# A two-layer graph network on one core: in the second layer a block's accumulator, query and softmax weights are placed in PSUM

## The chip, the core and the metric

The kernel runs on one NeuronCore of a Trainium2 chip. The engines have the names of the profile: PE multiplies matrices (PEld is its weight load), DVE (VectorE) and ACT (ScalarE)[...], POOL (GpSimd) here only issues DMAs, SP (SyncE) issues plain DMAs. The metric is the device time of one execution in microseconds. A change counts as measured here when it is above about 0.3%, and a verdict of faster or slower takes 2%.

## What is computed

Two graph layers over 6250 nodes and 100000 edges, with 128 channels, 8 heads of 16 channels, 16 node types and 32 edge types, then a linear map and a layer norm. Of one layer, this matters here:

```python
k, q, v = typed_linear(x, ntype, Wk), typed_linear(x, ntype, Wq), typed_linear(x, ntype, Wv)   # per node
kT = einsum('nhd,htdo->nhto', k, Watt); vT = einsum('nhd,htdo->nhto', v, Wmsg)                # per node and edge type
a = einsum('ehd,ehd->eh', kT[src, :, etype], q[dst]) * pri[:, etype].T / SQRT_D                # per edge and head
att = edge_softmax(a, dst, n)                                                               # over the edges of a node
hag = segment_sum(vT[src, :, etype] * att[:, :, None], dst)                                     # per node
h = silu(typed_linear(hag, ntype, Wa)); h = h * alpha + x * (1 - alpha); h = layernorm(h) * g + b
```

## The kernel before, in words

**Tables.** For each layer a table `tabs[l]` in HBM has, for each pair of node and edge type, one row of 256 values: the 128 of kT and the 128 of vT. The table of layer 0 is made in a first stage. That of layer 1 is made piece by piece while layer 0 goes over its edges (`nodes`, `pieces_of`, `table_block`): PE multiplies into PSUM tiles called `tb`, each a pair of banks of 512 values, of which the pool `tps` (line 780) has three. ACT copies them to SBUF and POOL scatters them (line 1183). All scatters must have landed before the first row of layer 1 is fetched. In layer 1 nothing is put into `tb`.

**Blocks and chunks.** Nodes are ordered by number of incoming edges and cut into 50 blocks of 128, one node a partition. Block b has KB[b] edge slots, and the blocks are grouped into 15 superblocks of 3 or 4 (`sbs`): 12 of one class of 4 node types each, and 3 mixed ones of all 16 types. A layer fetches 867 slots in all. Each fetch is an indirect DMA issued by POOL (line 966): it takes a column of 128 row numbers from the SBUF tile `ell` and brings 128 rows of 1 KB into `kv`. Four slots make a chunk; there are 12 buffers of a chunk.

**The order of the work** (`edges`, line 833). For each chunk of a block DVE multiplies the kT half by the block's query (line 978, `kv<-kv,q`) and sums each head's 16 products (line 982) into the scores `a`. Between these, one step of the generator `finished` runs, for the block before: scores masked (881), maximum (886), subtracted (888), exponential on ACT (890), sum (893), then chunk by chunk the vT half times its weight (901; the first chunk's product starts the accumulator `acc`), added to `acc` (908), and at the end the four partial sums of `acc` added up (911). Until then the `kv` buffers of the block before are held. So a block's rows are in use for about two blocks: with some 17 slots, or 5 chunks, in a block, about 10 of the 12 buffers.

After the last block of a superblock, `nodes` (line 1056) is spread as small pieces between the chunks: normalisation, typed linear map with masks `xm` made on DVE (line 232), tanh on ACT (line 1069), layer norm on DVE with a reciprocal root by iteration (1038 to 1042), and in layer 1 the final map and norm (1156 to 1169) and a scatter of the result by POOL (line 1216).

**Who sets the order.** POOL's queue is written out by hand (`manual_schedule(engines={Pool})`, line 1310); the instructions of the other engines are ordered by the framework's scheduler[...]. In layer 1 the queries come from HBM for a superblock at a time (`queries1`, line 827, tile `q` in SBUF), and `query(s, i)` (line 872) hands out the slice of a block, some chunks before that block starts.

In the kernel before, `q`, `a` (whose exponentials are written over the scores) and `acc` are SBUF tiles. So lines 978, 901 and 908 each have two SBUF inputs and one SBUF output.

## Time and profile before

| what | value |
|---|---|
| median of 3 runs | 3544.61 us (3541.61 to 3552.11) |
| the profiled execution | 3932.2 us, span 3930.4 us |
| first stage | 0 to 843 us |
| layer 0's edges (with the making of layer 1's table) | 843 to 2405 us |
| last scatters, nothing fetched | 2405 to 2497 us |
| layer 1's edges | 2497 to 3930 us |
| POOL over the span | 2104.1 us busy, 54% |
| DVE over the span | 2232.3 us busy, 57% |
| PE over the span | 1974.2 us busy, 50%, mean granted clock 0.697 |

How to read it: the profiled execution is longer than the timed ones, so its stages are compared with its own span, not with the median. The borders of the stages are the starts of the first fetch (line 966) of each layer and the last fetch of layer 0. "Busy" is the time in which an engine's records cover the clock; POOL's 0.30 us between two DMA issues is not in it. In the timeline, a row is start, duration, engine, line, operation, tiles, and in brackets the idle time before it and what ended it. Records of DVE overlap a little: one can start before the end of the one before.

### The profile page before, as it was taken

The numbers are of one execution on the slowest core, as the hardware profiler recorded it, in microseconds if no ns is written. First come the engines' busy times: TensorE is split into PE (matmuls) and PEld (weight loads), VectorE is DVE, ScalarE is ACT, GpSimd is POOL, SyncE is SP. The second block draws the span as 40 slices with busy tenths as digits, with TensorE's granted clock in tenths as the row PEclk, the third lists the DMA queues.
The fourth block names the chain that finished last, engine by engine and source line by source line (L and its number), as shares of the span: only waits on it lengthen the run. The fifth ranks groups of instructions, "written<-read, shape, count | busy, mean of one in ns | idle before, by whom it ended". The sixth has DMA issues, their size and how long they took to land. (4 is left out here: it accounts for less than half of the span.)

```text
span 3930.4 us, 25592 instructions
## 1 busy us (share of the span) xinstructions
PE 1974.2 (50%) x7142; PEld 887.1 (23%) x7142; DVE 2232.3 (57%) x4900; ACT 833.8 (21%) x1366; POOL 2104.1 (54%) x2032
## 2 busy tenths in 40 slices
PE   4999998950556367655766867202111122021212
PEld 2444553320222123222222323001010111010111
DVE  4787684424736456555745744346446465564746
ACT  1444434430123113421343144100000000000000
POOL 0000005637566566667556763476576676766764
PEclk9999999965667677677767777655555555555555
DMA  5676648793265346755566578533232233323321
GB/s 137 274 305 278 267 194 323 308 319 96 86 240 203 130 154 218 286 200 199 196 247 213 170 280 312 196 100 89 83 95 88 83 98 92 104 85 88 101 85 49
DMA packets 201147, 694.54 MB, mean 177 GB/s; under 512 B 61382, under 2 KB 111896, under 8 KB 175946
## 3 DMA queue, kind: packets, MB, share of 16 engines
q0 software_dynamic: 105424, 448.83, 34.2%
q1 hardware_dynamic: 72924, 234.11, 15.3%
q10 hardware_dynamic: 22642, 9.82, 1.1%
q8 instruction: 60, 0.98, 0.1%
q14 instruction: 97, 0.79, 0.1%
HBM read 268.12 MB, written 429.48 MB: 177 GB/s over the span
## 5 line engine op out<-in xcount | busy, mean ns | idle before, releaser
L966 POOL DMA_INDIRECT kv<-tab,ell x1734 | 1806.1, 1042 | 786.2 <-issue 501.0
L269 ACT COPY st<-tb 128x512 f32<-128x512 f32 (+1 forms) x976 | 683.1, 764 | 743.1 <-PE tb L262 458.4
L978 DVE TENSOR_TENSOR kv<-kv,q 128x512 f32<-128x512 f32 (+3 forms) x468 | 301.7, 647 | 469.2 <-DMA kv<-tab,ell 426.2
L732 PE MATMUL l<-xm,wkqv 128*128 128x512 f32 (+1 forms) x832 | 385.8, 599 | 54.8 <-DVE xm L232 54.8
L247 PE MATMUL nb<-ident,hag 128*128 128x128 f32 x100 | 25.4, 390 | 763.0 <-DVE hag L1014 350.1
L232 DVE SCALAR_TENSOR_TENSOR xm<-ntb,nb 128x384 f32<-128x384 bf16 (+1 forms) x336 | 186.7, 593 | 245.2 <-remote 158.4
L982 DVE TENSOR_REDUCE a<-kv 128x32 f32<-128x512 f32 (+3 forms) x468 | 297.2, 639 | 29.4 <-remote 6.5
L262 PE MATMUL tb<-bdv,kvT 32*128 32x512 f32 x800 | 276.5, 817 | 43.5 <-ACT st L269 24.8
L241 PE MATMUL nb<-xm,wa 128*128 128x384 f32 (+1 forms) x384 | 219.1, 731 | 151.2 <-DVE xm L232 91.0
L262 PE MATMUL tb<-bdk,kvT 32*128 32x512 f32 x800 | 256.4, 814 | 57.8 <-ACT st L269 35.5
L890 ACT ACTIVATE a<-a 128x128 f32<-128x128 f32 (+12 forms) x100 | 31.9, 319 | 1143.3 <-DVE a L888 487.1
L1183 POOL DMA_INDIRECT tab<-st,row x100 | 110.2, 1102 | 306.7 <-ACT st L269 265.7
L908 DVE TENSOR_TENSOR acc<-kv,acc 128x512 f32<-128x512 f32 (+3 forms) x368 | 233.2, 634 | 57.7 <-remote 47.6
L901 DVE TENSOR_TENSOR kv<-kv,a 128x512 f32<-128x512 f32 (+3 forms) x368 | 231.0, 636 | 0.0
L267 DVE COPY st<-tb 128x512 f32<-128x512 f32 (+1 forms) x208 | 149.2, 718 | 121.9 <-PE tb L262 88.4
L732 PEld LDWEIGHTS l<-xm,wkqv 128*128 128x128 f32 x832 | 149.0, 193 | 286.7 <-issue 199.1
L232 DVE SCALAR_TENSOR_TENSOR xm<-ntb,hT 128x512 f32<-128x512 int32 (+1 forms) x208 | 133.8, 658 | 139.7 <-PE l L732 102.1
L247 PE MATMUL nb<-ident,hs 128*128 128x128 f32 x100 | 32.1, 456 | 353.8 <-DVE hs L1094 274.9
L241 PE MATMUL nb<-xm,wq 128*128 128x384 f32 (+1 forms) x192 | 104.3, 704 | 179.4 <-DVE xm L232 159.1
L247 PEld LDWEIGHTS nb<-ident,hag 128*128 128x128 f32 x100 | 15.2, 193 | 781.7 <-issue 568.2
L720 POOL DMA_DIRECT2D ntb<-in_node_type_dram x13 | 7.3, 558 | 341.9 <-DVE xm L232 341.9
L262 PE MATMUL tb<-bdv,yT 32*128 32x512 f32 x784 | 169.7, 658 | 4.7 <-ACT st L269 3.5
(234 smaller groups left out, 2678.0 us busy)
## 6 DMA issues: line engine op xcount, KB each, us to landing
tab<-st SPq DMA_DIRECT2D x98, 2048.0 KB
kv<-tab,ell POOLq DMA_INDIRECT x1734
hr<-xrd SPq DMA_DIRECT2D x20, 192.0 KB
xrd<-xr POOLq DMA_DIRECT2D x11, 256.0 KB
hr<-in_x_dram POOLq DMA_DIRECT2D x10, 256.0 KB
ntb<-in_node_type_dram POOLq DMA_DIRECT2D x10, 256.0 KB
hr<-xrd SPq DMA_DIRECT2D x10, 256.0 KB
ntb<-typed SPq DMA_DIRECT2D x20, 96.0 KB
```

The lines of the kernel that those rows point to most:

```text
L232: nc.vector.scalar_tensor_tensor(xm[:, :n], ntb[:, :n], float(t), hT[:, :n], op0=ALU.is_equal, op1=ALU.mult)
L241: nc.tensor.matmul(ps[:, :n], w[:, t, :], xm[:, :n], start=(t == types[0]), stop=(t == types[-1]))
L262: nc.tensor.matmul(pt[:, b], yT[s, i * P:(i + 1) * P], bd[s, tt, :], start=True, stop=True)
L267: nc.vector.tensor_copy(to, pt)
L269: nc.scalar.copy(to, pt)
L732: nc.tensor.matmul(ps[i][:, :n], wkqv[:, i, t, :], xm[:, :n], start=(t == 0), stop=(t == TY - 1))
L901: nc.vector.tensor_tensor((v if j else acc).rearrange("p k (h d) -> p k h d", h=H), v.rearrange("p k (h d) -> p k h d", h=H), av[:, j0:j1, ...
L908: nc.vector.tensor_tensor(acc[:, :j1 - j0], kvt[j - 1][:, :j1 - j0, D:], acc[:, :j1 - j0], op=ALU.add)
L966: get = nc.gpsimd.indirect_dma_start(out=kv[:, j - j0, :], out_offset=None, in_=tabs[l][:], in_offset=bass.IndirectOffsetOnAxis(ap=ell[:, ...
L978: nc.vector.tensor_tensor(kk, kk, q.unsqueeze(1).to_broadcast([P, c, D]), op=ALU.mult)
L982: nc.vector.tensor_reduce(a[:, j0:j1, :], kk.rearrange("p k (h d) -> p k h d", h=H), axis=AX.X, op=ALU.add)
L1183: put = nc.gpsimd.indirect_dma_start(out=tabs[1].rearrange("(n t) c -> n (t c)", t=16), out_offset=bass.IndirectOffsetOnAxis(ap=row2[:, tg ...
```

## The change

It concerns layer 1 only (`l == 1`); layer 0 goes on as before. `query` takes a tile `tb` from the pool of bank pairs, [128, 2, 512] values, and has ACT copy the block's query into the first 128 values of its second bank. Line 978 reads the query from there. In `finished`, the exponentials are written behind the query in that bank (K times 8 values), not over the scores in SBUF; the sum of line 893 and the products of line 901 read them there. `acc` is the first bank of the pair. Nothing else differs: the same DVE instructions in the same number on the same sizes, and 50 more copies on ACT.

```diff
             def query(s, i):
-                return got[s][0][:, i, :]
-
-            def finished(s, i, chunks, kvt, a, sums, den):
+                if l == 0:
+                    return got[s][0][:, i, :], None
+                pair = tps.tile([P, 2, SB * P], F32, name="tb")
+                nc.scalar.copy(pair[:, 1, :D], got[s][0][:, i, :])
+                return pair[:, 1, :D], pair
+
+            def finished(s, i, chunks, kvt, a, pair, sums, den):
...
                 nc.vector.tensor_tensor(av, av, m.unsqueeze(1).to_broadcast([P, K, H]),
                                         op=ALU.subtract)
-                nc.scalar.activation(av, av, AF.Exp)
-                yield
-                yield
-                nc.vector.tensor_reduce(den[:, i, :], av.rearrange("p k h -> p h k"),
+                w = av if l == 0 else pair[:, 1, D:D + K * H].rearrange("p (k h) -> p k h", h=H)
+                nc.scalar.activation(w, av, AF.Exp)
+                yield
+                yield
+                nc.vector.tensor_reduce(den[:, i, :], w.rearrange("p k h -> p h k"),
                                         axis=AX.X, op=ALU.add)
 
-                acc = ep.tile([P, CH, D], F32, name="acc", bufs=1)
+                if l == 0:
+                    acc = ep.tile([P, CH, D], F32, name="acc", bufs=1)
+                else:
+                    acc = pair[:, 0].rearrange("p (k c) -> p k c", k=CH)
...
                         nc.vector.tensor_tensor(
                             (v if j else acc).rearrange("p k (h d) -> p k h d", h=H),
                             v.rearrange("p k (h d) -> p k h d", h=H),
-                            av[:, j0:j1, :].unsqueeze(3).to_broadcast([P, j1 - j0, H, HS]),
+                            w[:, j0:j1, :].unsqueeze(3).to_broadcast([P, j1 - j0, H, HS]),
                             op=ALU.mult)
...
             before = iter(())
-            q = query(0, 0)
+            q, pair = query(0, 0)
...
-                    before = finished(s, i, chunks, kvt, a, sums, den)
-                    q = then[0] if then else None
+                    before = finished(s, i, chunks, kvt, a, pair, sums, den)
+                    q, pair = then[0] if then else (None, None)
```

## The prediction

> **What bounds the kernel now.** The page's chain of waits breaks off after the last stores, so I read the sums by stage first, with borders at the first and last fetch of each layer. The change touches the last row alone.

> ```profile
> core 0: us, PE busy (x) PEld busy (x) DVE busy (x) ACT busy (x) POOL busy (x), PEclk, DMA share, GB/s
> 843.00:2405.00 1562.00, 916.04 (x2623) 377.32 (x2623) 879.63 (x1922) 417.60 (x554) 997.53 (x954) 0.70 0.58 200
> 2497.00:3931.00 1434.00, 256.51 (x642) 146.63 (x642) 803.28 (x2082) 46.03 (x126) 959.09 (x917) 0.53 0.31 89
> ```

> In the second layer (1434 us) the DMA engines are 31% busy, ACT hardly works, and POOL with 959 us is ahead of DVE with 803. Next, the groups of that stretch:

> ```profile
> L966 POOL DMA_INDIRECT kv<-tab,ell x867 | 905.6, 1045 | 402.4 <-issue 254.4 <-DVE acc L901 63.8 <-DVE hs L1083 15.1
> L1216 POOL DMA_INDIRECT out_dram<-o,node x50 | 53.5, 1070 | 73.8 <-DVE o L1169 61.0 <-issue 10.7 <-DVE a L888 0.9
> ...
> L978 DVE TENSOR_TENSOR kv<-kv,q 128x512 f32<-128x512 f32 x200 | 137.4, 687 | 250.3 <-DMA kv<-tab,ell 234.3 <-issue 15.9
> L982 DVE TENSOR_REDUCE a<-kv 128x32 f32<-128x512 f32 x200 | 135.3, 676 | 7.4 <-issue 2.1 <-remote 1.5 <-DVE m L886 1.3
> L908 DVE TENSOR_TENSOR acc<-kv,acc 128x512 f32<-128x512 f32 x150 | 102.7, 684 | 26.4 <-remote 24.1 <-issue 2.2
> ```

> POOL's account: 905.6 + 53.5 us in DMA records, 254.4 + 10.7 us of "issue" (0.30 us between two, the same everywhere), together 1224 us or 85% of the stretch; the other 210 us it waits, mostly for DVE to free `kv` (63.8 us, line 901) or to give a result (61.0 us, line 1169). DVE waits 234 us for fetched rows. So POOL's issue rate is the bound for most of the layer, with some stops that DVE causes.

> A fetch takes 1045 ns on average, but its median is 946. The timeline shows what the long ones are:

> ```profile
> 3209.64 0.68 DVE L901 TENSOR_TENSOR acc<-kv,a 128x512 f32<-128x512 f32 x1
> 3210.23 0.69 DVE L901 TENSOR_TENSOR kv<-kv,a 128x512 f32<-128x512 f32 x1
> 3210.31 3.23 POOL L966 DMA_INDIRECT kv<-tab,ell  x1 [0.30 <-issue]
> 3210.84 0.69 DVE L978 TENSOR_TENSOR kv<-kv,q 128x512 f32<-128x512 f32 x1
> 3211.44 0.69 DVE L901 TENSOR_TENSOR kv<-kv,a 128x512 f32<-128x512 f32 x1
> 3212.04 0.69 DVE L908 TENSOR_TENSOR acc<-kv,acc 128x512 f32<-128x512 f32 x1
> 3212.64 0.68 DVE L982 TENSOR_REDUCE a<-kv 128x32 f32<-128x512 f32 x1
> ...
> 3219.37 1.93 DVE L232 SCALAR_TENSOR_TENSOR xm<-ntb,nb 128x384 f32<-128x384 bf16 x4
> ...
> 3220.24 0.94 POOL L966 DMA_INDIRECT kv<-tab,ell  x1 [0.30 <-issue]
> ```

> The fetch that starts at 3210.31 lasts 3.23 us: to within 0.05 us until the row of DVE instructions with two SBUF inputs (lines 901, 978, 901, 908) gives way to the reduction of line 982 at 3212.64, plus an undisturbed 0.94. The fetch at 3220.24 starts amid four masks, which read one input from PSUM (`nb`), and takes 0.94. Over both layers I sorted the fetches and POOL's other indirect DMAs by what DVE did beside them: 126 beside only reductions (over 0.4 us) averaged 0.953 us, 61 beside masks (over 0.8 us) 0.970, 111 beside more than 1.3 us of two-input instructions 1.90. DVE's own instructions show no such stretching (line 978 lies between 675 and 709 ns).

> **The change, part by part.** *Removed: the stretching.* In the second layer 867 x (1045 - 946) ns = 86 us. All but some 6 us belong to lines 978, 901 and 908; other instructions still have two SBUF inputs (881, 888, 1014, 1090, 1094, the root's small ones). For each DMA start I took the remainder of the two-input row that it fell into: 226 us for all of them, 15 us for these others alone, so 15/226 of 86. Leaves 80 us of POOL's time.

> [...] By the rows it is 80 us; the 3.23 us fetch decides for the rows. A fetch takes its row numbers from SBUF (`ell`), which is a read.

> *What of the 80 us reaches the end.* I split all POOL DMAs of the layer (92 us over 946 ns, stores included): 47 us lie in 208 DMAs within 15 us after a stop of POOL, where DVE catches up in dense rows, and 45 us in the 709 others. The calm part counts in full: there DVE waits for rows. Of the other part some can be lost again in the next stop. So 45 to 86 in the profiled execution of 3932.2 us (span 3930.4); I take 70, making it about 3862. The timed runs are 388 us shorter. POOL's records and gaps are even, and its stops sum to some 620 us over both layers; so what is shorter there is likely the stops, and POOL is the bound for more of the time, which favours the upper end. With fewer stops there are fewer dense rows: the calm rate, 45/709 x 917, gives 58. I keep 70 for the median: 3545 - 70 = 3475.

> *Moved: operands to PSUM.* 752 DVE instructions get a PSUM operand: 234 of line 978, 234 of 901, 184 of 908, 50 each of 911 and 893. [...] The rows say nothing of it: line 1083 with a PSUM input takes 344 ns as line 1094 without does, line 1050 takes 286 from `nb` and 281 from `hs`: 0 to 4 us. I take the rows. No row shows DVE writing PSUM (234 instructions) or reading and writing the same bank (184 of line 908): above, I bound it by a doubling of the 0.60 us from start to start of two of them, 184 x 0.6 = 110 us; below, line 911 (1000 ns where line 982 needs 676 for as many values in unbroken order) might lose its 0.32 us, -16 us. I take 0, nearest to the rows with PSUM inputs. What hides it is DVE's 234 us of waiting for rows; without that cover it would count in full.

> *Added: 50 copies on ACT* (128x128), as long as the exponential of that size, 309 ns: 15 us on an engine with 46 of 1434 us busy. Its exponentials now write PSUM; no row shows ACT doing so. Bounds -5 and +5 us for 50 of them; I take 0, on an idle engine.

> *Added: a wait.* Line 978 of a block's first chunk waits for the copy. Behind it on DVE stands everything, and POOL waits for the buffers that DVE frees. The copy stands in ACT's queue behind tanh (line 1069) and the copy of line 1156, which wait for PE. Below nothing is excluded: it adds a step. Above: DVE's longest wait for tanh in this layer is 4.9 us (16.1 us in 6); once for each of 15 superblocks is 75 us of DVE. The query is asked for some steps before the block ends, and DVE has spare time, so I take 0. The bank pair itself is free: three pairs, two blocks in work, and the tables are finished before. POOL and SP queues get nothing new.

> **The rivals.**
> - *Freed (0.68):* as above, 3475; its own range 3445 to 3515.
> - *Swallowed (0.15):* POOL's stops for DVE (210 us) are set by DVE and PE, and grow by what the fetches save. For it: 47 of the 92 us lie behind such stops. Against: the 234 us that DVE waits for rows. Gives about 3540.
> - *Slower, by the copy's wait (0.11):* the copy is late at each block start. DVE's cover is 234 - 80 = 154 us; the gain is gone from (154 + 80)/50 = 4.7 us a block. At 6 us a block, 300 - 234 = 66 us are lost: about 3610. For it: ACT[...] waits up to 58 us for PE. Against: few of those waits have a query behind them.
> - *It does not do what it says (0.06):* an instruction with one input in PSUM still holds POOL off, because it reads and writes `kv` in place. Against: the masks' 0.970 us. Gives 3545.

> **How the numbers follow.** 0.3% (10.6 us) is about what a measurement of this kernel can tell from no change. Faster: all of the first and a little of the second, 0.71; within: 0.15; slower: the third and edges of the others, 0.14. The range 3445 to 3555 takes in the first case, the second and the fourth, and leaves out the slow one and the tails.

> **What would show it.** Right: in the second layer line 966 averages 950 to 965 ns, no fetch of 2 us or more beside lines 978, 901, 908, while the first layer keeps its long ones; that layer is 60 to 85 us shorter; lines 978 and 901 stay within 10 ns of 687. Swallowed: short fetches, but more than 250 us of POOL waiting for DVE. Slower: waits of line 978 for ACT's copy, several us long. Wrong in the sizes: line 908 far above 684 ns, or line 911 off its 1000.

## The result, and the profile after

The changed kernel takes 3498.2 us in the median of 4 runs (3493.8 to 3504.2), beside 3548.4 for the one before: ratio 0.9866, 95% interval 0.984 to 0.9892. By the ratio that is 47.5 us less, 38 to 57 by its interval: more than the 0.3% that this kernel's measurement can tell, though less than the 2% that counts as faster. 3475 had been predicted.

The first profile of before shows an execution that was held up for some 390 us: DVE and ACT each wait 384 us for updates of semaphores that came late (its rows with "<-remote", of which the later profiles have none). So the stages below are compared with a second profile of the same kernel, the first experiment. It had its own clean span, 3533.9 us. By stage, the second layer of the second profile of before, and then of after:

```profile
2273.00:3534.00 1261.00, 246.04 (x642) 145.74 (x642) 795.11 (x2082) 46.26 (x126) 931.18 (x917) 0.54 0.35 101
```

```profile
core 0: us, PE busy (x) PEld busy (x) DVE busy (x) ACT busy (x) POOL busy (x), PEclk, DMA share, GB/s
2286.00:3493.00 1207.00, 246.32 (x642) 145.66 (x642) 773.49 (x2082) 57.37 (x173) 874.21 (x917) 0.54 0.36 105
```

The last of the (x) pairs is POOL: 57.0 us less of it for the same 917 DMAs, and the stage is 54 us shorter. What runs ahead of that layer is left alone by the change; it took 2274 us in one profile and 2286 in the other, the first layer 1349 and 1355 of it. So the gain of the stage is POOL's, nearly one for one. The groups say of which instructions; POOL in the second layer of before (second profile), and of after, where line 966 has become 976:

```profile
L966 POOL DMA_INDIRECT kv<-tab,ell x867 | 877.0, 1011 | 284.9 <-issue 248.4 <-DVE acc L901 8.5 <-DVE acc L908 3.4
L1216 POOL DMA_INDIRECT out_dram<-o,node x50 | 54.2, 1084 | 46.6 <-DVE o L1169 32.0 <-issue 11.3 <-DVE a L982 1.5
```

```profile
L976 POOL DMA_INDIRECT kv<-tab,ell x867 | 823.5, 950 | 284.2 <-issue 243.2 <-DVE tb L911 7.6 <-DVE ri L1052 4.4
L1226 POOL DMA_INDIRECT out_dram<-o,node x50 | 50.7, 1014 | 50.1 <-DVE o L1179 35.4 <-issue 10.1 <-DVE rd L1019 1.5
```

A fetch fell from 1011 to 950 ns, which is the undisturbed 946 but for 4. POOL's idle time has hardly grown, from 331.5 us to 334.3: what the fetches save is not waited away. Now DVE: four of its groups before (second profile), then the same stretch of after. Lines 988, 992, 911, 918 and 921 are the former 978, 982, 901, 908 and 911; `tb` is the bank pair.

```profile
L978 DVE TENSOR_TENSOR kv<-kv,q 128x512 f32<-128x512 f32 x200 | 138.1, 690 | 414.1 <-DMA kv<-tab,ell 395.6 <-issue 18.3
L908 DVE TENSOR_TENSOR acc<-kv,acc 128x512 f32<-128x512 f32 x150 | 102.1, 681 | 0.0
L901 DVE TENSOR_TENSOR kv<-kv,a 128x512 f32<-128x512 f32 x150 | 102.1, 687 | 0.0
L911 DVE TENSOR_REDUCE sums<-acc 128x128 f32<-128x512 f32 x50 | 49.9, 997 | 0.0
```

```profile
L988 DVE TENSOR_TENSOR kv<-kv,tb 128x512 f32<-128x512 f32 x200 | 137.4, 687 | 381.7 <-DMA kv<-tab,ell 370.3 <-issue 11.1
L992 DVE TENSOR_REDUCE a<-kv 128x32 f32<-128x512 f32 x200 | 135.7, 679 | 0.2
L918 DVE TENSOR_TENSOR tb<-kv,tb 128x512 f32<-128x512 f32 x150 | 104.6, 698 | 0.1
L911 DVE TENSOR_TENSOR kv<-kv,tb 128x512 f32<-128x512 f32 x150 | 99.2, 677 | 0.1
L911 DVE TENSOR_TENSOR tb<-kv,tb 128x512 f32<-128x512 f32 x50 | 34.4, 689 | 0.1
L921 DVE TENSOR_REDUCE sums<-tb 128x128 f32<-128x512 f32 x50 | 34.1, 683 | 0.0
```

With an operand in PSUM the DVE products and sums take the same time, between 10 ns less and 17 ns more. Two reductions got faster: the one at the end (line 911), from 997 to 683 ns, and the sum of the exponentials (line 893, now 900), whose 50 took 19.5 us and take 14.8. DVE still waits 370 us for rows. The timeline of after has the counterpart of the 3.23 us fetch, two fetches that start amid a dense row of the changed instructions:

```profile
3176.49 0.69 DVE L911 TENSOR_TENSOR tb<-kv,tb 128x512 f32<-128x512 f32 x1
...
3176.73 0.94 POOL L976 DMA_INDIRECT kv<-tab,ell  x1 [0.30 <-issue]
3177.10 0.42 DVE L988 TENSOR_TENSOR kv<-kv,tb 128x256 f32<-128x256 f32 x1
...
3177.44 1.14 DVE L911 TENSOR_TENSOR kv<-kv,tb 128x512 f32<-128x512 f32 x2
...
3177.98 0.95 POOL L976 DMA_INDIRECT kv<-tab,ell  x1 [0.30 <-issue]
```

Both take their 0.95 us. Counted over the whole layer, it is the rule. In the second profile of before, 213 fetches begin while DVE is inside line 978, 901 or 908; 148 of them take more than 0.06 us over 0.946, and the 213 have 48.6 of the 56.8 us that all fetches take over it. In after, 248 fetches begin inside the same three instructions, and none takes more than 0.03 us over.

The wait that the change added, line 988 for ACT's copy, would be a row in the list of DVE's waits (who waited for whom, us in total, times, longest). Its head, for the second layer of after:

```profile
DVE kv L988 <- DMA kv<-tab,ell: 381.1, 159, 19.8
DVE bn L1060 <- PE nb L1172: 21.9, 10, 7.1
DVE kv L988 <- issue: 11.1, 9, 2.4
DVE th L1086 <- ACT th L1079: 9.1, 6, 4.8
```

There is none, nor is there one in the whole list. ACT makes the copies in 269 ns each, and each is done at least 3.4 us (21 us in the median) before line 988 of its block starts.

### The profile page after: what moved, and what is told of

It is laid out like the page before. It is cut to its first block, busy times and chain, and to the rows that moved or that the text cites. A ratio compares the mean times of both kernels' runs of the same rounds, so it can differ in the third digit from the quotient of the medians.

```text
span 3492.4 us, 25642 instructions
## 1 busy us (share of the span) xinstructions
PE 1941.9 (56%) x7142; PEld 883.3 (25%) x7142; DVE 2203.0 (63%) x4900; ACT 843.2 (24%) x1416; POOL 2013.0 (58%) x2032
## 5 line engine op out<-in xcount | busy, mean ns | idle before, releaser
L976 POOL DMA_INDIRECT kv<-tab,ell x1734 | 1723.5, 994 | 612.2 <-issue 472.5
L988 DVE TENSOR_TENSOR kv<-kv,tb 128x512 f32<-128x512 f32 (+3 forms) x234 | 151.3, 647 | 392.6 <-DMA kv<-tab,ell 381.1
L988 DVE TENSOR_TENSOR kv<-kv,q 128x512 f32<-128x512 f32 (+3 forms) x234 | 151.8, 651 | 372.7 <-DMA kv<-tab,ell 364.8
L241 PE MATMUL nb<-xm,wa 128*128 128x384 f32 (+1 forms) x384 | 211.9, 716 | 108.4 <-DVE xm L232 108.1
L232 DVE SCALAR_TENSOR_TENSOR xm<-ntb,hT 128x512 f32<-128x512 int32 (+1 forms) x208 | 133.9, 659 | 146.4 <-PE l L732 108.7
L232 DVE SCALAR_TENSOR_TENSOR xm<-ntb,nb 128x384 f32<-128x384 bf16 (+1 forms) x336 | 186.0, 593 | 62.1 <-PE nb L247 26.8
L878 ACT COPY tb<-q 128x128 f32<-128x128 f32 x50 | 13.5, 269 | 574.5 <-DVE sums L921 426.2
L241 PEld LDWEIGHTS nb<-xm,wa 128*128 128x128 f32 x384 | 96.6, 263 | 219.6 <-DVE xm L232 133.7
```

Of the source, the lines that this page charges most:

```text
L232: nc.vector.scalar_tensor_tensor(xm[:, :n], ntb[:, :n], float(t), hT[:, :n], op0=ALU.is_equal, op1=ALU.mult)
L241: nc.tensor.matmul(ps[:, :n], w[:, t, :], xm[:, :n], start=(t == types[0]), stop=(t == types[-1]))
L878: nc.scalar.copy(pair[:, 1, :D], got[s][0][:, i, :])
L976: get = nc.gpsimd.indirect_dma_start(out=kv[:, j - j0, :], out_offset=None, in_=tabs[l][:], in_offset=bass.IndirectOffsetOnAxis(ap=ell[:, ...
L988: nc.vector.tensor_tensor(kk, kk, q.unsqueeze(1).to_broadcast([P, c, D]), op=ALU.mult)
```

## The experiments

The theory: a POOL DMA that starts while DVE runs instructions with two SBUF inputs is held by them; an operand in PSUM ends that, and since POOL's issue rate bounds the layer, its time is the kernel's. The expectations call it the port theory; the runs show the holding, not by what in the hardware it comes about. The main rival: the gain comes from DVE, whose reduction of `acc` became shorter, so that buffers come free sooner.

**The kernel before once more**, nothing edited.

> The kernel before, unchanged, for a second profile. The first profile of before was 388 us longer than its timed runs, the profile after was not. If only that one execution was held up (updates of semaphores handed on late), this one has a span near 3545, the first layer's edges take about 1355 us as they do after (the change does not touch them), the second layer with its tail about 1255 to 1265 (206 were shown gained there: 1206 after plus about 50), and the stretching of POOL's DMAs in the second layer is nearer to the calm rate of the prediction, about 58 us, than to 92. Rival: profiling always costs this kernel 388 us and the change took that away; then the span is near 3930 again and the first layer near 1563.

Measured: span 3533.9 us, time 3535.8; first layer 1349 us, second with its tail 1260 us. The excess of POOL's DMAs over 946 ns, summed over the second layer's records, is 64 us (92 in the first profile). So the first profile's extra length belonged to that one execution, and a good part of its stretching with it.

**One operand at a time.** The three edits, each against the changed kernel:

```diff
 # query only
-                w = av if l == 0 else pair[:, 1, D:D + K * H]...
+                w = av
-                if l == 0:
+                if True:
                     acc = ep.tile([P, CH, D], F32, name="acc", bufs=1)
 # weights only
-                nc.scalar.copy(pair[:, 1, :D], got[s][0][:, i, :])
-                return pair[:, 1, :D], pair
+                return got[s][0][:, i, :], pair
-                if l == 0:
+                if True:
                     acc = ep.tile([P, CH, D], F32, name="acc", bufs=1)
 # accumulator only
-                nc.scalar.copy(pair[:, 1, :D], got[s][0][:, i, :])
-                return pair[:, 1, :D], pair
+                return got[s][0][:, i, :], pair
-                w = av if l == 0 else pair[:, 1, D:D + K * H]...
+                w = av
```

> Only the query lies in PSUM (copy on ACT, line 988 with one SBUF input); weights and accumulator stay in SBUF. Port theory (a DVE instruction with two SBUF inputs holds off a fetch that starts in it): rows of two-input instructions get shorter, fetches in the second layer average about 990 ns instead of about 1010, 10 to 25 us gained on before. Rival (the gain comes from DVE, whose reduction of acc fell from 1000 to 683 ns, so that buffers come free sooner): no gain, within 5 us of before, or a loss by the added wait for the copy.

> Only the softmax weights lie in PSUM (exponential written there, lines 900 and 911 read there); no query copy, accumulator in SBUF. Port theory: 10 to 25 us gained on before, fetches of the second layer shorter on average by 10 to 30 ns. Rival (DVE's shorter reduction): no gain, within 5 us of before.

> Only the accumulator lies in PSUM (lines 911 for the first chunk, 918 and 921), query and weights in SBUF. Port theory: line 918 stops holding POOL off, 10 to 25 us gained, and the three parts together gain about the whole 50 us, not exactly, since rows of two-input instructions are cut at different places. Rival (DVE's shorter reduction at line 921): this one alone gains nearly the whole 50 us, and its fetches stay near 1010 ns.

Measured, with POOL's busy time in the second layer from the groups (fetches and stores) and the stage's length from its first fetch to the end:

| kernel | ratio to before (95%) | fetch, ns | POOL busy, us | stage, us |
|---|---|---|---|---|
| before (second profile) | 1 | 1011 | 931.2 | 1260 |
| query only | 0.9947 (0.9927 to 0.9967) | 996 | 917.4 | 1247 |
| weights only | 0.9936 (0.9918 to 0.9955) | 989 | 908.2 | 1240 |
| accumulator only | 0.9908 (0.9889 to 0.9928) | 986 | 906.7 | 1237 |
| all three (after) | 0.9866 (0.984 to 0.9892) | 950 | 874.2 | 1206 |

Each part gains, and in each the stage is shorter by what POOL saved: 13.8, 23.0, 24.5 and 57.0 us of POOL beside 14, 21, 24 and 54 us of stage. The rival falls: the query gains without touching a reduction (DVE is busy 793 us in the layer, beside 795 before), and the accumulator alone brings the short reduction (673 ns at its line 920) but less than half of the stage's gain. The weights do shorten a reduction, the sum of line 893, but by 4.9 us in all.

The fetches say line by line where each gain comes from. In the second profile of before, those that begin inside the query's line (978) take 10.0 us in all over 0.946 us each, those inside the weights' line (901) 16.9 and those inside the accumulator's (908) 21.7. In each experiment the line whose operand moved is at 0.0 or 0.1 us, with 32, 100 and 80 fetches begun inside it, while the two others together keep 37, 24 and 31 us. The query gains least because the fewest fetches begin in its product: 38, beside 111 and 64.

The times themselves are less sharp. By the ratios the three parts gain 19, 23 and 33 us (10 to 25 had been expected of each), 74 in sum, where all three together gained 47.5 (38 to 57); POOL's savings add up better, 61 us beside 57. The execution in the second profile of before, 3535.8 us, is also shorter than all 11 executions of that kernel timed beside the three (3536.4 to 3561.4).

**More DVE work of either kind**, to part the second SBUF input from the load. In the changed kernel one more product for each chunk of the second layer, its result not used:

```diff
+                        if l == 1:
+                            extra = ep.tile([P, CH, D], F32, name="acc", bufs=1)
+                            nc.vector.tensor_tensor(
+                                extra[:, :c], kv[:, :c, D:],
+                                Q.unsqueeze(1).to_broadcast([P, c, D]), op=ALU.mult)
 # Q = got[s][0][:, i, :] (in SBUF)     or     Q = q (in PSUM)
```

> The changed kernel with one more DVE product per chunk in the second layer (234 in all, up to 128x512, its result not used), both inputs in SBUF: the query is taken from SBUF for it. About 234 x 0.55 = 130 us more of DVE, whose spare time in that layer is 370 us of waiting for rows. Port theory: fetches that start in these products are stretched again, 20 to 60 us in all, fetch mean of the second layer 975 to 1020 ns instead of 957 (950 over fetches alone), and the kernel is 20 to 60 us slower than after. Rival (only DVE's load counts): the same time as its twin with the query from PSUM.

> The twin: the same 234 more products, the query taken from PSUM, so one SBUF input. Port theory: DVE's spare time covers it, fetches stay near 950 ns, within 10 us of after (3498). Rival (only DVE's load counts): as slow as the twin with both inputs in SBUF.

Measured: with SBUF 3530.2 us, ratio to before 0.993 (0.9915 to 0.9944); with PSUM 3497.9 us, 0.9847 (0.9832 to 0.9861). DVE is busy alike, 902 and 900 us in the second layer. The load costs nothing that shows (3497.9 us beside 3498.2 for after); the second SBUF input costs 32 us, and the fetches show it: 985 ns on average against 953. With SBUF 92 fetches begin inside the extra product, 76 of them are stretched, and they lose 28.8 us; with PSUM 81 begin inside it, and none takes more than 0.003 us over. One of the stretched, in the timeline of the kernel with the extra product (line 992) from SBUF:

```profile
2610.82 0.69 DVE L988 TENSOR_TENSOR kv<-kv,tb 128x512 f32<-128x512 f32 x1 [2.52 <-DMA kv<-tab,ell]
2611.50 0.69 DVE L992 TENSOR_TENSOR acc<-kv,q 128x512 f32<-128x512 f32 x1
2611.64 1.37 POOL L976 DMA_INDIRECT kv<-tab,ell  x1 [0.30 <-issue]
2612.10 0.16 DVE L1053 TENSOR_TENSOR t<-ri 128x3 f32<-128x3 f32 x1
```

The fetch starts inside the product, 0.46 us before DVE's next instruction starts, and takes 0.42 us more than its 0.95.

**The first layer too.** Its fetches are still stretched after the change (1038 ns on average), but its bank pairs are in use for the table. Two ways to make room, against the changed kernel:

```diff
 # query and weights
-        tps = ctx2.enter_context(tc.tile_pool(name="tps", bufs=3, space=PSUM))
+        tps = ctx2.enter_context(tc.tile_pool(name="tps", bufs=2 if fast else 3, space=PSUM))
+        qps = ctx2.enter_context(tc.tile_pool(name="qps", bufs=2, space=PSUM)) if fast else None
-                if l == 0:
-                    return got[s][0][:, i, :], None
-                pair = tps.tile([P, 2, SB * P], F32, name="tb")
-                nc.scalar.copy(pair[:, 1, :D], got[s][0][:, i, :])
-                return pair[:, 1, :D], pair
+                pair = qps.tile([P, SB * P], F32, name="qw")
+                nc.scalar.copy(pair[:, :D], got[s][0][:, i, :])
+                return pair[:, :D], pair
-                w = av if l == 0 else pair[:, 1, D:D + K * H]...
+                w = pair[:, D:D + K * H]...
-                    acc = pair[:, 0]...
+                    acc = tps.tile([P, 2, SB * P], F32, name="tb")[:, 0]...
 # all three: qps as above, tps with 3 single banks (table_block with w=1), and
+        aps = ctx2.enter_context(tc.tile_pool(name="aps", bufs=1, space=PSUM)) if fast else None
+                acc = aps.tile([P, CH, D], F32, name="accp")
```

> Query and weights in PSUM in the first layer too, in two banks of their own; the accumulator in PSUM only in the second; the pool of pairs for the table has two, not three. Port theory: the first layer's stretching (90 us after) falls by about as large a share as query and weights took together in the second (37 of 64), some 45 us, and the first layer gets 30 to 50 us shorter, unless two pairs hold the table back (then POOL's waits of line 1193 or so for ACT grow and the gain is below 20 us). Time 3450 to 3480.

> All three in PSUM in both layers: two banks for query and weights, one for the accumulator, and three single banks for the table's products, which ACT then copies in twice as many instructions of half the size (595 instead of 1021 ns, some 65 us more of ACT of which 420 of 1355 us is busy in the first layer). Port theory: the first layer's stretching falls from 90 us to about 10; if POOL remains the bound there, the first layer gets 60 to 80 us shorter, time about 3425; if PE and ACT with single banks become the bound for the table, the gain is lost and the time is 3490 or more.

Measured: query and weights 3477.2 us, 0.9786 (0.9774 to 0.9799), which beats both kernels and is the only one here past 2%; all three 3515.4 us, 0.9895 (0.9878 to 0.9912), no better than after, whose interval it touches. With query and weights the first layer's fetches fall from 1038 to 973 ns and the layer from 1355 to 1314 us, as expected; but the pause before the second layer, in which the last pieces of the table are scattered, grows from 85 to 102 us, so 24 us are left in the profile. With all three the fetches are at 961 ns, but the layer is at 1356 us again and the pause at 111. POOL's waits in the first layer say why, after and then all three:

```profile
POOL kv L976 <- issue: 241.0, 752, 9.6
POOL tab L1193 <- ACT st L269: 114.4, 27, 25.1
```

```profile
POOL tab L1190 <- ACT st L269: 222.1, 48, 21.4
POOL kv L973 <- issue: 221.8, 725, 1.2
```

The scatter now waits 222 us for ACT's copies of the table, where it waited 114. There the time that the fetches gave back turned into a wait for the table. ACT in turn waits 329 us for PE's products of the table, where it waited 109: in single banks the same 1600 products keep PE busy for 823 us, in pairs for 528. The run changed the size of the tiles and the number of ACT's copies together, so which of the two costs the time stays open.

## Why the prediction was right, and what was mis-sized

*The bound.* POOL's share of the second layer had been read as 85%. Without the stops of the held-up execution it is (931 us of records + 917 x 0.30 us of gaps)/1261, or 96%. So what POOL saves is time.

*The stretching.* The cause was right: with the three lines' operands in PSUM the fetches have 3.3 us of excess left (6 had been forecast; with the stores 6.7), and the twin products show that the second SBUF input does it, not DVE's load (28.8 us lost by the fetches begun inside the extra product from SBUF, at most 0.003 us by any one begun inside that from PSUM). Of the fetches that began inside the three lines, 148 of 213 were stretched before (second profile), and none of 248 after. That it is the reading of the row numbers in `ell` which is held was argued; no run moved them.

How long a fetch is held was read from an uncommon case. The 3.23 us fetch waits for a whole row of instructions. In the second profile, 170 fetches are stretched by an instruction with two SBUF inputs, and 158 of them only until that one instruction ends, 40 us in all; 12 wait through more of them, 13 us. The prediction's own sum hinted at it: the remainders of the rows came to 226 us, the excess to 92. The forecast did not suffer, since it took the excess as measured. Line 978 is also less even than the prediction says: one of its 200 takes 620 ns, and in the second profile they lie between 671 and 751.

*"What of the 80 us reaches the end"* is the step that was mis-sized: 70 us, where POOL saved 57.0, the stage became 54 us shorter and the timed runs 47.5 (38 to 57). The 92 us of stretching that it started from came from the held-up execution. There 30 fetches waited through several instructions, for 48 us; in the second profile, with 64 us of stretching, 12 did, for 13 us. The better number stood beside it: the calm rate, 58 us. In the second profile that rate is 57.7, from 881 of the 917 DMAs; the 36 behind a stop add only 8 us. That 58 meets the 57.0 so closely is partly chance: it falls 6 us short of the 64 and counts the 6.7 that stayed. The prediction saw that the timed runs would have fewer stops and drew from that only that POOL is more the bound, which was so, but kept 70 between 58 and 80. Its sign that the layer would be 60 to 85 us shorter failed with it. Why the timed runs show 47.5 where the stage shows 54 is not known; 54 lies in their interval.

*Operands in PSUM, taken at 0.* Right for inputs: 687 ns beside 690 for the former line 978, and DVE's 795 us in the layer fell to 773. Writing: line 918, in place in one bank, takes 698 ns where 681 were needed, far from a doubling. The lower bound of -16 us for the final reduction came true: 50 x (997 - 683) ns. The sum of line 893, not thought of, gave another 5 us.

*The copies and their wait, taken at 0.* 269 ns each instead of 309, and no wait of line 988 for them.

*The rivals.* Swallowed: POOL's stops above 0.35 us sum to 44 us before (second profile) and 47 after, so at most 3 us were swallowed. Slower by the copy's wait: no such wait. Not doing what it says: the twin products exclude it.

## What to carry to other kernels

Where POOL's indirect DMAs set the pace, look at their mean against their median, and at what DVE does when a long one starts. Idle PSUM banks took the second operand of DVE's products here at no cost to DVE (795 us busy in the layer before, 773 after); where the banks had to come from the table's maker, part of the gain (17 of 41 us) or all of it went into waits. Before sizing a gain from a profile whose execution is much longer than the timed runs, take the rate from its calm stretches, and count how much of the rest lies behind stops that the timed runs do not have.
